# Planned durations of eight kinds of products, and the table of wanted times, in a kernel whose order of work is planned

## The chip, the cores and the metric

The kernel runs on one core of one Trainium2 chip, as one launch. The metric is the device time of a launch in microseconds (us). Before the change five runs took 1682.94 to 1686.12 us, with a median of 1685.28 us.

The core has five engines that matter here, each with a queue of its own that runs in the order written: TensorE (PE in the profile; PEld is its loading of weights), VectorE (DVE), ScalarE (ACT), GpSimd (POOL) and SyncE (SP, which starts most transfers).

## The reference, cut to what matters

A stream x of 64 sequences of 64 tokens of width 128 goes through four layers. Each layer adds, through a tanh gate, an attention to a context of width 96 and then a feed-forward part:

```python
x = x + tanh(g_xattn[0]) * L0_xattn(layernorm(x), ctx)      # 16 heads
x = x + tanh(g_ffn[0])   * L0_ffn(layernorm(x))             # 32 experts, 6 of them a token, and a shared one
x = x + tanh(g_xattn[1]) * L1_xattn(layernorm(x), ctx)      # 16 heads, clamp, NaN guard
x = x + tanh(g_ffn[1])   * L1_ffn(layernorm(x))             # 8 experts, 2 a token, and a shared one
x = x + tanh(g_xattn[2]) * L2_xattn(layernorm(x), ctx)      # 8 heads of 64
x = x + tanh(g_ffn[2])   * L2_ffn(layernorm(x))             # 8 experts, 2 a token, and a shared one
x = x + tanh(g_xattn[3]) * L3_xattn(ctx, layernorm(x), mask)  # resampler: 2 heads, keys of context and x
x = x + tanh(g_ffn[3])   * L3_ffn(layernorm(x))             # 4 experts, 2 a token, norms inside
```

All is float32. Attention stays inside a sequence, so blocks of sequences are independent of each other all the way down, except that layer 1's clamped attention has one NaN flag for all.

## The kernel before, in words

**Tiling.** The 4096 tokens are cut into 8 blocks of 512 (`NB`, `TOK`): four tiles of 128 tokens, 8 sequences. x stays in on-chip memory for the whole launch. A stage is one part of one layer for one block: `attention_16` (layers 0 and 1), `gated_ffn` (layers 0 and 2), `end_attention_1`, `sparse_ffn` (layer 1, for two blocks at a time, a group), `context_8` (keys and values of layer 2, which need x not at all, written to memory and read again), `attention_8`, `attention_lat` (layer 3) and `ffn_3`.

**Products.** Experts' weights are dense in layers 0 and 2: for each chunk of 128 hidden units TensorE makes g and u, ScalarE puts Silu on g (tile h), VectorE multiplies by u, GpSimd multiplies by the expert's weight pb in layer 0 (in layer 2 it scales the input beforehand), and TensorE adds the product to acc. The weights come from a route: logits (pl), scores and top-k on VectorE (tile c), a transpose (pcT), a copy (cT), a store to memory (cD) and a load that repeats one row over all partitions (pb). In layer 1 the route makes a table of slots (prank, then VectorE, then pid), GpSimd gathers the tokens (zs), the experts' weights come by transfers (wt), results go to memory (oD) and are gathered again (back). `ffn_3` makes its norm's variances by products (pg, pvar), then a transpose pt, a route (pcT with cr), a spread (pb, zs) and products ph and acc.

**Who decides the order.** No instruction is issued when the Python code reaches it. `Plan` records every operation (`note`), groups some into units that stay together (`unit`), and at the end `order` lays all of them on five queues in a list schedule: it steps through time, and an engine that is free takes, of the operations whose inputs are ready and whose tiles fit in the pools, the one with the smallest key. `issue` then writes the instructions in the order of their planned starts. The plan costs nothing on the chip: only the order remains of it, and each engine runs its own part of that order, waiting by semaphores for what it needs.

Two inputs of the plan are touched by the change. One is the planned duration of an operation: `_duration` works it out of engine and size, and `nc.unit(us)` puts a number in its place. So `with nc.unit(0.93, claim=[pr])` says that the four score products of a tile take TensorE 0.93 us. The units with a number are the scores (sc), the weighted sums (av) and the values (pv) of the attentions, pvar, and acc. The other is the key: `stage` gives each operation a wanted time between a start and an end, in proportion to the planned TensorE work of its stage done so far; start and end come from the table `TIMES`, by kind of stage and block. The numbers order the operations among each other; they need not be times that are kept.

Beside this the plan models hand-overs between engines (`HOP`), transfers, a port shared by VectorE and GpSimd, the change of ScalarE's function tables (`TABLE_LOAD`), a slower TensorE after a pause (`COLD`), and the number of buffers.

Since all instructions are issued by `bound(*args, **kw)` in `issue`, nearly all of them have one line in the profile, L435. They are told apart by the names of their tiles.

Of the kernel before, what the change touches and what calls it, by code (L numbers as in the profile page):

```python
# [47 lines left out]

TIMES = {
    "16 heads, 0": [  # L50
        (-54.5, 328), (250.4, 262.4), (374.9, 421.5), (506.5, 421.8),
        (569.6, 591.2), (622.8, 674.7), (713.4, 645.8), (778.3, 584.2),
    ],
    "16 heads, 1": [
        (333, 444.3), (423.8, 572.1), (557.3, 698.9), (649.7, 728.9),
        (528, 564.7), (824.1, 934.8), (897.1, 1004.8), (764.9, 1636.1),
    ],
    "8 heads": [
        (1784.4, -176.2), (1320.1, 880.9), (1496.5, 1065.9), (1635.3, 950.3),
        (1016.4, 1173.4), (1845.9, 1720.9), (1648.7, 1814.1), (2307, 1648.3),  # L60
    ],
    "context, 8 heads": [
        (-1147.3, -84.8), (477.4, 520.9), (377.6, 314.9), (633.9, 1171.7),
        (690.6, 791.4), (824, 1018.8), (1320.9, 1029), (1545.2, 1373.3),
    ],
    "end of 16 heads, 1": [
        (985.5, -185.1), (934.2, -12.1), (1624.5, 1208.6), (677.3, 370.2),
        (1548.3, 1684.6), (1613, 2357.5), (2268, 1506.6), (1257.7, 1182.8),
    ],
    "gated 0": [  # L70
        (374.1, 413.5), (399.2, 482.9), (487.5, 550.8), (555.8, 662.2),
        (639.4, 711.8), (705.7, 784.1), (771.6, 834.8), (824.4, 943.5),
    ],
    "gated 1": [
        (-14.1, 982.7), (998.8, 1329.4), (1464.1, 1777.1), (1740.3, 1898.3),
    ],
    "gated 2": [
        (-577.4, 810.8), (1063.5, 1347.3), (-255, 804.4), (709.7, 1264.9),
        (1127.4, 1220.7), (970.7, 1635.2), (271.5, 1477), (1190.9, 2021.9),
    ],  # L80
    "last": [
        (1168.5, 1372.8), (1313.9, 1442.4), (1334.7, 1838.8), (1476.8, 1489.4),
        (2151.3, 2352.2), (2115.9, 2719.1), (3058.2, 3370.9), (261.9, 602.3),
    ],
    "resampler": [
        (-938.8, 590.2), (409.2, 477.3), (251.8, 893.4), (1125.5, 1677.4),
        (-179.1, 1216.5), (691.6, 289.1), (1556.9, 1376.5), (684.3, 580.8),
    ],
}
AT_ONCE = {}  # L90
# [366 lines left out]
def flamingo_kernel(ctx: ExitStack, tc: tile.TileContext, a: dict, out: bass.AP):  # L457
    nc = Plan(tc)
# [285 lines left out]
    with nc.stage(0.0, 1.0):  # L744
        nc.gpsimd.memset(sums_w, 0.0)
        for i in range(2):
# [3 lines left out]
            t = tile_of([P, BB * 4, 2, 32], f"values{i}")  # L750
# [8 lines left out]
    def attention_16(layer, blk):  # L759
# [49 lines left out]
        def scores(pr, t):  # L809


            kb = tile_of([P, 2, 8, S], "kb")
            nc.gpsimd.tensor_mul(
                kb,
                kT[:, t * P : (t + 1) * P].rearrange("p (b s) -> p b s", s=S).unsqueeze(2).to_broadcast([P, 2, 8, S]),
                head8.unsqueeze(1).unsqueeze(3).to_broadcast([P, 2, 8, S]),
            )
            sc = ps_two("sc")
            with nc.unit(0.93, claim=[pr]):
                for b in range(2):  # L820
                    q0 = t * P + b * S
                    for h in range(2):
                        nc.tensor.matmul(
                            sc[b * 64 : (b + 1) * 64, h, :],
                            lhsT=qT[h * 64 : (h + 1) * 64, q0 : q0 + S],
                            rhs=kb[h * 64 : (h + 1) * 64, b, :, :],
                            start=True,
                            stop=True,
                        )
            sc_h = sc.rearrange("p h (j s) -> p (h j) s", s=S)  # L830
            top = tile_of([P, 16], "top")
            if layer == 1:

                T = blk * TB + t
                nc.scalar.activation(pr, sc_h, AF.Tanh, accum_out=seen[:, T : T + 1])
            nc.vector.tensor_reduce(top, sc_h, axis=AX.X, op=ALU.max)
            wide = top.unsqueeze(2).to_broadcast([P, 16, S])
            if layer == 1:

                nc.vector.tensor_scalar(top, top, CLAMP, -CLAMP, op0=ALU.min, op1=ALU.max)  # L840
                nc.vector.scalar_tensor_tensor(pr, sc_h, -CLAMP, wide, op0=ALU.max, op1=ALU.subtract)
                nc.vector.tensor_scalar_min(pr, pr, 0.0)
            else:
                nc.vector.tensor_tensor(pr, sc_h, wide, op=ALU.subtract)
            flat = pr.rearrange("p h s -> p (h s)")
            nc.scalar.activation(flat, flat, AF.Exp, scale=scale)
            done.append(len(nc.ops) - 1)

        def weighted(pr, t, acc_tile):

            acc = acc_tile.rearrange("p (i n) -> p i n", i=2)
            prT = tile_of([P, 8, P], "prT")
            for g in range(2):
                pt = ps("pt")
                transposed(
                    pt, [pr[:, 2 * j : 2 * j + 2, :].rearrange("p h s -> p (h s)") for j in range(4 * g, 4 * g + 4)],
                    claim=[prT, acc_tile],
                    behind=done[t | 1],
                )
                nc.scalar.copy(prT[:, 4 * g : 4 * g + 4, :].rearrange("p j q -> p (j q)"), pt)  # L860
            with nc.unit(1.2):
                for b in range(2):
                    cols_b = slice(t % 2 * P + b * 64, t % 2 * P + (b + 1) * 64)
                    for odd in range(2):
                        for c in range(4):
                            nc.tensor.matmul(
                                acc[32 * c : 32 * c + 32, 0, cols_b],
                                lhsT=of_pair(v[:, (2 * t + b) * 4 + c, :, :], odd),
                                rhs=prT[:, 2 * c + odd, b * 64 : (b + 1) * 64],
                                start=(odd == 0),  # L870
                                stop=(odd == 1),
                            )
                for odd in range(2):
                    for c in range(4):
                        nc.tensor.matmul(
                            acc[32 * c : 32 * c + 32, 1, t % 2 * P : (t % 2 + 1) * P],
                            lhsT=of_pair(sums_w, odd),
                            rhs=prT[:, 2 * c + odd, :],
                            start=(odd == 0),
                            stop=(odd == 1),  # L880
                        )
            if t % 2:
                rs = tile_of([P, 2 * P], "rs")
                nc.vector.reciprocal(rs, acc[:, 1, :])
                nc.vector.tensor_mul(yT[:, (t - 1) * P : (t + 1) * P], acc[:, 0, :], rs)
# [84 lines left out]
    def attention_8(blk):  # L970
# [22 lines left out]
        def softmax(pair):  # L993

            sc = ps_two("sc8")
            pr = tile_of([P, 8, 2, S], "pr8")
            with nc.unit(1.35, claim=[pr]):
                for t in range(2):
                    for j in range(4):
                        for h in range(2):  # L1000
# [26 lines left out]
        def weighted(pair, pr):  # L1027
            for t in range(2):
# [2 lines left out]
                transposed(pt, [pr[:, 4 * t + j, :, :].rearrange("p h s -> p (h s)") for j in range(4)], claim=[prT])  # L1031
                nc.scalar.copy(prT.rearrange("p j q -> p (j q)"), pt)
                av = ps("av8")
                with nc.unit(1.25, claim=[yT[2 * pair + t]]):
                    for b in range(2):
                        for j in range(4):
                            for h in range(2):
# [45 lines left out]
    def attention_lat(blk):  # L1083
# [19 lines left out]
        v = tile_of([P, BB, P], "v3")  # L1103
        for g in range(2):
            pv = ps("pv3")
            with nc.unit(1.05, claim=[v]):
                for b in range(4 * g, 4 * g + 4):
                    for h, (src, w) in enumerate(((cT, w3kv), (lT, w3lkv))):
                        nc.tensor.matmul(
                            pv[h * 64 : (h + 1) * 64, b % 4 * P : (b % 4 + 1) * P],  # L1110
                            lhsT=src[:, b * S : (b + 1) * S],
                            rhs=w[:, P : 2 * P],
                            start=True,
                            stop=True,
                        )
# [5 lines left out]
            )  # L1121
        sc = ps_two("sc3")
        pr = tile_of([P, 2, TB, P], "pr3")
        with nc.unit(1.3, claim=[pr, low]):
            for t in range(TB):
                for h in range(2):
                    hs = slice(h * 64, (h + 1) * 64)
# [26 lines left out]
            nc.scalar.copy(prT[:, h, :, :].rearrange("p t q -> p (t q)"), pt)  # L1154
        av = ps("av3")
        yT = tile_of([P, TOK], "yT3")
        with nc.unit(1.4, claim=[yT]):
            for t in range(TB):
                for b in range(2):
                    for h in range(2):  # L1160
# [170 lines left out]
    def gated_ffn(layer, blk):  # L1331
# [9 lines left out]
        for n, (i, who) in enumerate(chunks):  # L1341
# [17 lines left out]
            nc.vector.tensor_mul(h, h, u)  # L1359
            if who is not None and layer != 2:  # L1360
                nc.gpsimd.tensor_mul(h, h, pb)
            with nc.unit(0.95):
                nc.tensor.matmul(acc, lhsT=w2[:, w], rhs=h, start=(n == 0), stop=(n == len(chunks) - 1))
        add_to_x(blk, tokens_again(acc), gate_f(layer))

# [153 lines left out]
    def sparse_ffn(group):  # L1519
# [13 lines left out]
        for blk, zT in zip(blocks, zTs):  # L1533
            acc = ps("acc")
            for ch in range(chunks):
# [7 lines left out]
                    nc.tensor.matmul(u, lhsT=shared_w[:, 1, w], rhs=zT, start=True, stop=True)  # L1543
                nc.scalar.activation(h, g, AF.Silu)
                nc.vector.tensor_mul(h, h, u)
                with nc.unit(0.95):
                    nc.tensor.matmul(acc, lhsT=shared_w[:, 2, w], rhs=h, start=(ch == 0), stop=(ch == chunks - 1))
            add_to_x(blk, tokens_again(acc), gate_f(1))
        oD = dram.tile([SLOT_TILES * P, D], F32, tag="oD", name="oD")
# [127 lines left out]
    def ffn_3(blk):  # L1677
# [39 lines left out]
        for i in range(8):  # L1717
# [2 lines left out]
            with nc.unit(claim=[h, acc]):  # L1720
                nc.tensor.matmul(ph, lhsT=w1[:, i * P : (i + 1) * P], rhs=zs[i // 2], start=True, stop=True)
            nc.scalar.activation(h, ph, AF.Relu)
            with nc.unit(0.95):
                nc.tensor.matmul(acc, lhsT=w2[:, i * P : (i + 1) * P], rhs=h, start=(i == 0), stop=(i == 7))
        po = tokens_again(acc).rearrange("p (t d) -> p t d", d=D)
        mv, r = moments([po[:, t, :] for t in range(TB)], "on")
# [153 lines left out]
```

## Time and profile before

| | |
|---|---|
| median of 5 runs | 1685.28 us (1682.94 to 1686.12) |
| the profiled execution's own time | 1682.23 us |
| its span, first to last instruction | 1680.4 us |
| mean granted TensorE clock | 0.972 |
| TensorE busy | 1565.9 us (93%), 12737 instructions |
| VectorE busy | 1069.0 us (64%) |
| GpSimd busy | 969.5 us (58%) |
| ScalarE busy | 883.1 us (53%), of it 163 loads of function tables, 209.1 us |
| transfers | 180.74 MB, 108 GB/s on average |

The span is what the profile covers; the time of the execution has 1.83 us around it. Busy time of TensorE is the time in which some product is under way: products overlap, so a product's duration in the profile (603 ns for half of a 128x512 float32 product, which goes through the array in two passes) is longer than the distance from its start to the next one's. The granted clock is the share of full speed that the chip let TensorE run at; it is seen to switch between full and half. "A wait" is idle time of an engine ahead of an instruction, put down to the operation that ended it.

### The profile page before, as it was taken

The page shows a single profiled execution, that of the slowest core. Times are in us where ns is not written, and L with a number is a line of the kernel's source. Part 1 is how long each engine was busy: PE and PEld are TensorE (multiplying, and loading weights), DVE is VectorE, ACT ScalarE, POOL GpSimd, SP SyncE. Part 2 cuts the span into 40 slices and gives each one's busy share as a digit, 9 for nine tenths or more (in the row PEclk, how much of TensorE's full clock was granted, in tenths as well). Part 3 has the DMA queues.
Part 4 walks back from the last instruction along what each step waited for, and adds up shares of the span by engine and source line. Part 5 has one row for each costly group of instructions (what it writes and reads, how often), then busy time and mean ns, then how long its engine had stood idle before and what let it go on. Part 6 is the DMA issues. An engine that isn't in the chain of part 4 may idle for free.

```text
span 1680.4 us, 34191 instructions
## 1 busy us (share of the span) xinstructions
PE 1565.9 (93%) x12737; PEld 938.9 (56%) x12737; DVE 1069.0 (64%) x2932; ACT 883.1 (53%) x1325; POOL 969.5 (58%) x986
## 2 busy tenths in 40 slices
PE   5999999999999999998959999999999997999987
PEld 2645444454554554556848766757467665664543
DVE  3865577677867656676467657665766545665563
ACT  2654667676767645753325537565446543453522
POOL 8374655664564655523275768665478555955651
PEclk9999999999999999997979999999999999999998
DMA  7232234422321313134758554131344624121001
GB/s 236 93 109 65 77 94 152 128 91 68 78 94 49 111 44 120 54 133 157 209 188 219 183 163 133 60 110 40 119 133 123 214 24 159 38 77 51 33 15 56
DMA packets 107774, 180.74 MB, mean 108 GB/s; under 512 B 22964, under 2 KB 53016, under 8 KB 103128
## 3 DMA queue, kind: packets, MB, share of 16 engines
q1 hardware_dynamic: 102488, 168.06, 30.7%
q0 software_dynamic: 5120, 10.50, 3.2%
q8 instruction: 101, 1.65, 0.4%
q14 instruction: 65, 0.53, 0.1%
HBM read 146.71 MB, written 35.26 MB: 108 GB/s over the span
## 4 chain that ended last, share of the span: by engine, by line
PE 43%; POOL 7%; DMA 4%; DVE 4%; issue 2%; ACT 1%; SPq 0%; DVEq 0%; POOLq 0%; ACTq 0%
PE acc L435 7%; PE g L435 6%; PE u L435 6%; PE po L435 5%; PE pt L435 3%; PE av L435 3%; PE ph L435 2%; POOL z L435 2%; POOL back L435 2%; PE pv L435 2%; PE pk L435 2%; PE sc L435 2%; PE pq L435 1%; PE pg L435 1%; PE pz L435 1%
## 5 line engine op out<-in xcount | busy, mean ns | idle before, releaser
L435 POOL TENSOR_TENSOR h<-h,pb 128x512 f32<-128x512 f32 x128 | 162.2, 1281 | 181.3 <-DVE h L435 117.5
L435 DVE TENSOR_TENSOR h<-h,u 128x512 f32<-128x512 f32 x224 | 150.4, 683 | 180.1 <-PE u L435 133.1
L435 ACT ACTIVATE h<-g 128x512 f32<-128x512 f32 x224 | 132.2, 597 | 213.4 <-PE g L435 185.8
L435 ACT ACT_TABLE_LOAD x163 | 209.1, 1283 | 24.2 <-PE g L435 10.8
L435 POOL TENSOR_TENSOR ln_r<-ln_ve,minus_half 128x4 f32<-128x4 f32 x64 | 66.5, 1038 | 176.0 <-DVE ln_ve L435 173.5
L435 DVE TENSOR_REDUCE top<-sc 128x16 f32<-128x1024 f32 x80 | 97.3, 1217 | 82.2 <-PE sc L435 55.8
L435 POOL TENSOR_TENSOR kb<-kT,masks 128x1024 f32<-128x1024 f32 x64 | 121.3, 1909 | 41.5 <-ACT kT L435 30.2
L435 PE MATMUL u<-zTm,w_L 128*128 128x512 f32 x272 | 141.3, 602 | 2.0 <-DVE h L435 1.3
L435 PE MATMUL g<-zTm,w_L 128*128 128x512 f32 x272 | 141.6, 603 | 0.5 <-DVE h L435 0.5
L435 POOL DMA_INDIRECT zs<-zD,z_rows x96 | 95.8, 998 | 75.9 <-DVE z_rows L435 45.0
L435 PE MATMUL acc<-h,w_L 128*128 128x512 f32 x272 | 138.3, 608 | 0.0
L435 PE MATMUL acc<-h,L_w 128*128 128x512 f32 x272 | 135.2, 600 | 2.8 <-ACT h L435 2.1
L435 ACT COPY prT<-pt 128x512 f32<-128x512 f32 x176 | 96.3, 592 | 45.4 <-PE pt L435 45.0
L435 POOL TENSOR_TENSOR pb<-zTm,pb 128x512 f32<-128x512 f32 x64 | 81.9, 1304 | 50.6 <-DMA pb<-cD 44.8
L435 PEld LDWEIGHTS pt<-masks,pr 128*128 128x128 f32 x704 | 82.6, 143 | 48.3 <-issue 34.3
L435 ACT ACTIVATE pr<-pr 128x1024 f32<-128x1024 f32 x88 | 93.1, 1058 | 20.4 <-DVE pr L435 19.5
L435 PE MATMUL pt<-masks,pr 128*128 128x128 f32 x704 | 97.8, 280 | 1.6 <-POOL pr L435 1.6
L435 POOL DMA_INDIRECT back<-oD,rows_of x64 | 65.0, 1015 | 40.0 <-DMA oD<-zs 17.9
L435 DVE SCALAR_TENSOR_TENSOR x<-po,gates,x 128x512 f32<-128x512 f32 x56 | 41.7, 747 | 69.1 <-PE po L435 68.9
L435 PEld LDWEIGHTS u<-zTm,w_L 128*128 128x128 f32 x272 | 48.5, 191 | 58.1 <-issue 47.3
L435 PEld LDWEIGHTS g<-zTm,w_L 128*128 128x128 f32 x272 | 48.3, 190 | 57.8 <-issue 45.7
L435 POOL TENSOR_SCALAR z<-x,ln_mv,ln_r 128x128 f32<-128x128 f32 x96 | 76.8, 810 | 1.5
(300 smaller groups left out, 3490.6 us busy)
## 6 DMA issues: line engine op xcount, KB each, us to landing
wt<-experts SPq DMA_DIRECT2D x96, 384.0 KB
pb<-cD SPq DMA_DIRECT2D x256, 128.0 KB
pb<-cD SPq DMA_DIRECT2D x96, 256.0 KB
k_d<-kS SPq DMA_DIRECT2D x8, 1024.0 KB
v_d<-vS SPq DMA_DIRECT2D x8, 1024.0 KB
kT<-k_d SPq DMA_DIRECT2D x8, 1024.0 KB
v<-v_d SPq DMA_DIRECT2D x8, 1024.0 KB
oD<-zs SPq DMA_DIRECT2D x32, 192.0 KB
```

Of the source, the lines that this page charges most:

```text
L435: bound(*args, **kw)
```

## The change

Eight kinds of units get other planned durations, and `TIMES` gets other numbers throughout. Nothing else is edited: the operations, the tiles and the pools are the same.

| unit | TensorE products in it | units | before | after |
|---|---|---|---|---|
| sc, 16 heads | 4 | 64 | 0.93 | 1.10 |
| av, 16 heads | 24 | 64 | 1.20 | 1.10 |
| sc8, 8 heads | 32 | 16 | 1.35 | 1.20 |
| av8, 8 heads | 16 | 32 | 1.25 | 1.17 |
| pv3, resampler | 8 | 16 | 1.05 | 0.97 |
| sc3, resampler | 16 | 8 | 1.30 | 1.10 |
| av3, resampler | 16 | 8 | 1.40 | 1.17 |
| acc, all feed-forward parts | 1 | 288 | 0.95 | 0.86 |

```diff
 TIMES = {
     "16 heads, 0": [
-        (-54.5, 328), (250.4, 262.4), (374.9, 421.5), (506.5, 421.8),
-        (569.6, 591.2), (622.8, 674.7), (713.4, 645.8), (778.3, 584.2),
+        (-218.9, 180.8), (96.9, 222.5), (494.2, 524.3), (583.8, 558.6),
+        (674.4, 696.1), (725.7, 776.3), (814.1, 744.9), (887.2, 748),
     ],
...
     "last": [
-        (1168.5, 1372.8), (1313.9, 1442.4), (1334.7, 1838.8), (1476.8, 1489.4),
-        (2151.3, 2352.2), (2115.9, 2719.1), (3058.2, 3370.9), (261.9, 602.3),
+        (1294.4, 1457.3), (1383.4, 1568.8), (1409.3, 1950), (1146.2, 1322.8),
+        (2328, 2565.4), (1954.4, 2831.2), (2475.5, 3606.3), (-348.4, 879.3),
     ],
...
-            with nc.unit(0.93, claim=[pr]):
+            with nc.unit(1.1, claim=[pr]):
...
-            with nc.unit(1.2):
+            with nc.unit(1.1):
...
-            with nc.unit(1.35, claim=[pr]):
+            with nc.unit(1.2, claim=[pr]):
...
-                with nc.unit(1.25, claim=[yT[2 * pair + t]]):
+                with nc.unit(1.17, claim=[yT[2 * pair + t]]):
...
-            with nc.unit(1.05, claim=[v]):
+            with nc.unit(0.97, claim=[v]):
...
-        with nc.unit(1.3, claim=[pr, low]):
+        with nc.unit(1.1, claim=[pr, low]):
...
-        with nc.unit(1.4, claim=[yT]):
+        with nc.unit(1.17, claim=[yT]):
...
-            with nc.unit(0.95):
+            with nc.unit(0.86):
```

The last edit is made at three places: `gated_ffn`, the shared expert of `sparse_ffn`, and `ffn_3`. All ten kinds of stages in `TIMES` have new numbers for all their blocks.

In the issued program the same instructions stand in another order on every queue. With equal neighbours merged, TensorE's queue has 1863 rows before and 1853 after; VectorE's 2149 and 2137, ScalarE's 1055 and 1041, GpSimd's 548 and 551, SyncE's 663 and 662, and on each many of the rows moved. Only the loads of ScalarE's function tables change in number, from 163 to 156.

## The prediction

> **What bounds the kernel now.** First the head of the page and its slices over time: is one engine full, and where is it not?
>
> ```profile
> span 1680.4 us, 34191 instructions
> PE 1565.9 (93%) x12737; PEld 938.9 (56%) x12737; DVE 1069.0 (64%) x2932; ACT 883.1 (53%) x1325; POOL 969.5 (58%) x986
> PE   5999999999999999998959999999999997999987
> PEclk9999999999999999997979999999999999999998
> ```
>
> TensorE is busy 93% of the span and nothing else comes over 64%. So the span is TensorE's work plus the holes in it: 1680.4 - 1565.9 = 114.5 us of holes, and some time in which its clock is low. The holes sit at the start, at slices 18 to 21 and at the end. The windows of 40 us put numbers on them (columns: stretch, its length, then busy time and count of PE, PEld, DVE, ACT, POOL, then the granted clock, DMA share and GB/s):
>
> ```profile
> 0.00:40.00 40.00, 20.97 (x120) 9.85 (x120) 13.99 (x52) 11.37 (x18) 33.29 (x49) 0.95 0.77 237
> 80.00:120.00 40.00, 36.32 (x150) 16.31 (x149) 29.61 (x82) 20.15 (x29) 31.79 (x38) 0.96 0.31 93
> 360.00:400.00 40.00, 37.46 (x306) 19.02 (x306) 28.28 (x77) 26.75 (x37) 27.17 (x29) 0.96 0.12 40
> 840.00:880.00 40.00, 22.74 (x97) 16.84 (x97) 26.63 (x114) 9.81 (x15) 29.51 (x29) 0.70 0.57 197
> 1400.00:1440.00 40.00, 30.53 (x88) 14.34 (x87) 18.43 (x62) 10.39 (x16) 31.47 (x31) 0.91 0.45 162
> ```
>
> In the other stretches TensorE is at 36 to 40 of 40 us. What ends the holes is told by the waits of TensorE (total us, times, longest):
>
> ```profile
> PE pid L435 <- DVE match L435: 15.5, 2, 10.2
> PE pcT L435 <- DVE c L435: 8.3, 3, 3.7
> PE g L435 <- POOL pb L435: 8.2, 2, 7.9
> PE pt L435 <- DMA zs<-zD,z_rows: 6.6, 4, 4.4
> PE pbias L435 <- DMA L_gate<-in_L_gate: 5.7, 1, 5.7
> PE pvar L435 <- DVE q L435: 5.5, 2, 4.9
> ```
>
> Each is a routing chain (pid: slots of experts; pcT: expert weights; g after pb: weights spread over partitions; pvar: variances) that had too few other products queued behind its start. I call the sum of the products that stand in TensorE's queue between the start of such a chain and the product that waits for its end its **cover**. Covers are counted from the order of the queue with distances from the timeline: 0.86 us for a 128x512 product (u at 82.24, g at 83.11), 0.44 for four transposes (po at 81.37, pc at 81.81), 1.02 for four sc products (sc at 30.93, pc at 31.95).
>
> **The change, part by part.**
>
> *The durations.* They enter no instruction. In the plan they take off about 31 us of TensorE's work: 288 acc products x 0.09 = 25.9, the attention kinds 16.1, and sc gives 64 x 0.17 = 10.9 back. On the chip both kernels have the same 7113 products, 695 transfers of SP and 160 indirect ones of POOL. TensorE's work term is 0.
>
> *The table of ScalarE's functions* is loaded 156 times instead of 163: 7 x 1.283 us (ACT_TABLE_LOAD, 209.1 us for 163) = 9.0 us of an engine that is 53% busy. Taken as 0; if it stood on the path, -9.0.
>
> *The order* changes on every queue (TensorE, VectorE, ScalarE, GpSimd, SyncE). I compare covers at each hole.
>
> (a) Start. pbias, which waits for the fourth gate matrix, stands third in the queue before and behind pv after. These rows show what it held up:
>
> ```profile
> 15.63 0.56 PE L435 MATMUL pbias<-L_gate,shift 128*128 128x4 f32 x2 [5.73 <-DMA L_gate<-in_L_gate]
> 16.05 1.07 PE L435 MATMUL pc<-masks,c_in 128*96 128x128 f32 x4
> 27.41 0.60 PE L435 MATMUL pz<-masks,z 128*128 128x128 f32 x4
> 13.50 0.21 ACT L435 ACTIVATE gates<-rows 128x8 f32<-128x8 f32 x1 [11.47 <-DMA rows<-in_rows]
> 7.57 2.73 POOL L435 TENSOR_SCALAR c_in<-c_in,cn_mv,cn_r 128x96 f32<-128x96 f32 x4
> ```
>
> The centred c_in is there at 10.30, so pc can start 5.7 us earlier; but the copy cn is queued on ScalarE behind gates, which ends at 13.71, where it was at 17.15. So the front moves by 3.4, less 0.4 for pbias further on: -3.0. pz, at 27.41 - 3.0 = 24.4, is behind the end of z (18.9) still. Bounds: -5.7 and 0 (a later transfer takes over; SP's c_in load goes behind two context loads of 0.4 us, and its user is blocks away).
>
> (b) Layer-0 routes (eight). Covers between pl and pcT were 8.8, 7.0, 8.5, 7.5, 8.9, 9.3, 7.9, 14.4 us and become 11.2, 33.7, 13.1, 10.7, 20.9, 8.9, 8.8, 8.2. The chain's own VectorE work is about 7.2 us. Other VectorE work put inside it now is 3.7, 2.6 and 10.1 us in routes 2, 3 and 5, which have the covers for it. The two that waited (3.68 us in 80:120, 3.08 in 280:320) gain 2.4 and 3.2 of cover: -5.5. Bounds -6.8 and 0.
>
> (c) Layer-2 routes. The two that waited (1.41 and 1.55 us) get 1.0 and 1.9 more; two others lose 2.2 and 0.3 (to 3.0 and 3.7, where 4.1 is needed): -2.5 + 1.5 = -1.0. Bounds -3.0 and +2.
>
> (d) The hole of 7.92 us at 1407, in the last pair's routing. From pcT (1405.62) to g (1415.17) 9.55 us pass with 1.3 of products, and eight back gathers of 1.25 each stand on GpSimd ahead of pb. After, all 16 gathers come before the route, and 6.4 us of products, attention's av8 among them, lie inside. Of those, pt must itself wait for the softmax (cover 4.7 us, its chain 8.0): 3.3. So 7.92 - 3.3 = -4.6. Bounds -7.9 and 0.
>
> (e) Sparse groups 0 and 1: cover from prank to pid 4.3 to 5.2 and 0.9 to 2.6. In group 1 the gathers follow on GpSimd after 16 back gathers, so there the cover from the last po of group 0 to pt counts: 10.3 to 11.2. -0.9 each: -1.8. Bounds -4 and +1.
>
> (f) One hand-over pcT to ph: cover 5.3 to 9.5, and 1.3 us of wait go: -1.3 (-1.3 to 0).
>
> (g) The end. Before, the last attention output po starts at 1614.44 and the span ends 65 us after po, with 37.6 us of products in between. After, 34.9: 2.7 move ahead. But both last pcT-to-ph covers are now small (1.4 to 0.9 and 11.2 to 0.4 us), and a pcT-to-ph chain took 8.7 (1631.24 to 1639.91). By hand, counted from po: ph 7.4, pz 10, pg to 16.4, pvar 20.8, pt 23.5, pcT 28.3, ph 36, last acc 50 to 51.5, and then the 10.2 us that follow it now: 60 to 62. Against 65, less the 2.7: -0.3 to -2.3; I take -1.0. Bounds -3 and +6 (the last cover lost in full).
>
> (h) What is new. Chains counted alone, without queues: in TensorE positions 30 to 400 the products with less cover than their chain go from 6 to 28, missing 1.1 us before and 7.7 after. Before, such short ones in the first 600 us cost about what they miss (sc 0.86, u 1.26), so +5.0. Two attention transposes late in the kernel miss 1.6 and 1.5: +3.1. Bounds 0 and +20: products with under 1 us to spare go from 460 to 519, and 59 x 0.35 us (half of a plain hand-over, as ACT o to po 0.68) is 20.
>
> (i) The clock. 80:120 is at 0.96 with its hole, 1.6 us lost, and 280:320 likewise; 1400:1440 at 0.91, 3.6 us. With b and d half of this 6.8 comes back, 3.4, and the clock that short new waits cost is taken at 1.4: -2.0 (-6 to +3). For the new ones 360:400 is the row: 0.96 with no hole over 1.53 us, two of which follow close. The Trainium skill (TensorE: Matmul & The Clock Gate, Why this matters for your kernels) asks only for no idle gaps above about 3 us, and by it the new short waits would cost no clock; the window 360:400 differs, and the measurement decides. By the page the sum below would be -13.5; by the row it stays.
>
> Sum: -3.0 - 5.5 - 1.0 - 4.6 - 1.8 - 1.3 - 1.0 + 5.0 + 3.1 - 2.0 = -12.1 us. The profiled execution took 1682.23 us, 1.83 around the span, and stands 3.05 under the median 1685.28 of the runs; against it 1670.1, and against the median **1673 us**.
>
> **The rivals.**
>
> 1. Slower: the tighter queue decides. Other engines run in the order written, and a late VectorE result holds the queue behind it. Price: h at its upper end, +20 instead of +8.1, and the gains b and d half spent on it (+5): -12.1 + 11.9 + 5 = +5, and with the end at its upper bound (+7) +12: 1690 to 1697. It decides from about 0.3 us a product in those 59. For it: 22 products more in positions 30 to 400 have less cover than their own chain. Against: they miss 0.3 us each on average, and the stages 120 to 700 run at 36 to 40 of 40 us.
>
> 2. No change: one local optimum against another. The missing cover summed over all chains is 75.8 us before and 77.1 after, and sc's new 1.10 is over its distance of 1.02, so not all durations are the chip's: 1685 within 3.4.
>
> 3. Faster than forecast: new short waits are taken up by the queues (h at 0 to 2) and the clock stays up: -12.1 - 7 - 3 = -22: 1663.
>
> **How the numbers follow.** Forecast 0.50, range 1667 to 1681; rival 1 0.21, rival 2 0.11, rival 3 0.18. A difference of under 0.2% (3.4 us) can't be told from none here. Faster: 0.50 + 0.18 = 0.68; same 0.11; slower 0.21. The range for 8 in 10 leaves out the far half of rival 1 and of rival 3: 1657 to 1693.
>
> **What would show it.** Right: no wait at pbias before pc, pz before 25; no pcT wait over 1.5 us in the first 650 us; the 7.92 us hole under 4; TensorE idle near 100 us. At the end a wait of 5 to 8 us before the last ph and before the second but last. Wrong: many waits of 0.2 to 1 us in 30 to 400 with VectorE or ScalarE as releaser (rival 1), or DVE-bound slices that were not there. The weakest step is h: covers tell of chains alone, not of the queues of four engines.

## The result: slower, and the profile after

The changed kernel takes 1694.08 us (median; 1685.26 to 1702.5), the kernel before 1684.93 us in the same comparison: a ratio of 1.0054, 95% interval 1.0043 to 1.0064. It is slower by about 9 us, where 12 us of gain were forecast. The profiled execution spans 1692.9 us against 1680.4, with a mean granted clock of 0.967 against 0.972.

The head of the page and two of its rows over time:

```profile
span 1692.9 us, 34168 instructions
...
PE 1569.3 (93%) x12737; PEld 945.1 (56%) x12737; DVE 1071.9 (63%) x2932; ACT 872.8 (52%) x1318; POOL 963.6 (57%) x986
...
PE   6999999999999999998969889999999998999976
...
PEclk9999999999999999988969999999999999999988
```

TensorE is busy 3.4 us longer for the same products, which goes with its lower clock, and idle for 1692.9 - 1569.3 = 123.6 us instead of 114.5. Of the windows, four of the stretches shown of before and one more (columns as there):

```profile
0.00:40.00 40.00, 23.57 (x150) 11.35 (x154) 15.89 (x54) 13.14 (x21) 34.82 (x49) 1.00 0.79 242
80.00:120.00 40.00, 38.54 (x154) 18.45 (x153) 30.75 (x111) 23.01 (x33) 29.14 (x31) 1.00 0.43 139
360.00:400.00 40.00, 38.08 (x190) 16.33 (x189) 31.02 (x72) 32.25 (x45) 18.97 (x15) 1.00 0.29 94
960.00:1000.00 40.00, 32.68 (x334) 24.59 (x333) 26.47 (x85) 18.48 (x28) 27.88 (x29) 0.91 0.49 152
1400.00:1440.00 40.00, 34.51 (x383) 21.72 (x382) 31.82 (x120) 16.03 (x26) 31.73 (x34) 0.99 0.19 57
```

The places that the prediction named did get better: 80 to 120 by 2.2 us, 1400 to 1440 by 4.0. Longer windows show where TensorE is idle instead. The last column is a second profile of the same changed kernel, taken with the experiments; it tells how far one profile can be trusted:

| stretch, us | before | after | after again |
|---|---|---|---|
| 0 to 120 | 23.2 | 21.2 | 22.0 |
| 120 to 720 | 9.2 | 16.6 | 16.1 |
| 720 to 960 | 31.6 | 30.6 | 31.3 |
| 960 to 1080 | 4.7 | 11.2 | 7.5 |
| 1080 to 1440 | 18.1 | 11.0 | 10.2 |
| 1440 to the end | 27.8 | 33.0 | 34.4 |

The waits of TensorE (total us, times, longest):

```profile
PE ph L435 <- DVE zs L435: 15.6, 2, 8.0
PE pid L435 <- DVE match L435: 13.4, 2, 8.1
PE pt L435 <- DMA zs<-zD,z_rows: 12.4, 8, 4.7
PE sc L435 <- DVE pr L435: 10.9, 11, 2.6
...
PE pcT L435 <- DVE c L435: 5.1, 5, 1.6
PE pt L435 <- POOL pr L435: 4.4, 9, 1.2
```

The long route waits shrank (pcT from 8.3 to 5.1, pid from 15.5 to 13.4). New are the two waits of ph at the end, twice as much waiting for gathered tokens (zs, 6.6 before; 8.9 in the second profile), and many small ones: sc had 4.1 us in 4 waits.

Idle time alone does not place the loss, because the stretches hold different work. A point that both orders reach with almost the same work behind them is the first pid, which begins the slots of layer 1: 6096 product records of 12737 are done there before, 6071 after. From there to the end, before and then after:

```profile
771.90:1680.40 908.50, 837.27 (x6642) 565.20 (x6642) 543.00 (x1708) 415.65 (x657) 546.99 (x580) 0.96 0.37 114
```

```profile
771.80:1692.90 921.10, 844.87 (x6666) 572.28 (x6666) 550.21 (x1709) 411.87 (x655) 541.51 (x580) 0.95 0.37 113
```

Up to the first pid the two kernels take the same time, 771.9 and 771.8 us (774.2 in the second profile): after is idle 4.1 us more there and busy 4.1 us less. The whole 12.5 us between the two spans lie behind it: 5.0 us more idle time, and 7.6 us more of busy time for nearly the same products. So the change did two things, and they have to be explained apart: in the first stages its gains were eaten up, and in the later ones it lost time.

### The profile page after: what moved, and what is told of

Read it like the earlier page. It is cut to its first block, busy times and chain, and to the rows that moved or that the text cites. A ratio compares the mean times of both kernels' runs of the same rounds, so it can differ in the third digit from the quotient of the medians.

```text
span 1692.9 us, 34168 instructions
## 1 busy us (share of the span) xinstructions
PE 1569.3 (93%) x12737; PEld 945.1 (56%) x12737; DVE 1071.9 (63%) x2932; ACT 872.8 (52%) x1318; POOL 963.6 (57%) x986
## 3 DMA queue, kind: packets, MB, share of 16 engines
q8 instruction: 101, 1.65, 0.4%
## 4 chain that ended last, share of the span: by engine, by line
PE 68%; DVE 11%; POOL 7%; issue 5%; DMA 5%; ACT 3%; SPq 1%; POOLq 0%; DVEq 0%; ACTq 0%
PE acc L435 13%; PE g L435 11%; PE u L435 11%; PE pt L435 5%; PE po L435 5%; PE av L435 5%; PE sc L435 4%; PE ph L435 3%; PE pk L435 3%; PE pv L435 2%; DVE top L435 2%; DVE pr L435 2%; PE pq L435 2%; DMA pb<-cD 2%; POOL z L435 1%
## 5 line engine op out<-in xcount | busy, mean ns | idle before, releaser
L435 DVE RECIPROCAL rs<-av 128x256 f32<-128x256 f32 x32 | 56.1, 1753 | 40.1 <-PE av L435 40.1
L435 PE MATMUL ph<-zs,L_w 128*128 128x512 f32 x128 | 66.6, 644 | 15.6 <-DVE zs L435 15.6
L435 PE MATMUL sc<-kb,qT 64*64 64x512 f32 x512 | 70.2, 618 | 11.5 <-DVE pr L435 7.3
```

## The experiments

**The suspect in the first stages.** Between 120 and 720 us the waits of TensorE name ScalarE and VectorE tiles one by one, mostly for 1 to 3 us. One step further back they have something in common. ScalarE's waits for GpSimd's h in this stretch, before and after:

```profile
ACT h L435 <- POOL h L435: 4.6, 4, 2.3
...
ACT zTm L435 <- POOL h L435: 1.5, 1, 1.5
...
ACT zTs L435 <- POOL h L435: 1.1, 1, 1.1
```

```profile
ACT h L435 <- POOL h L435: 11.4, 4, 4.1
...
ACT qT L435 <- POOL h L435: 6.8, 3, 3.2
```

7.2 us before, 18.2 after. The timeline of after at the longest of them (start, duration, engine, operation, idle time before it and what ended that):

```profile
437.13 3.12 POOL L435 TENSOR_SCALAR z<-x,ln_mv,ln_r 128x128 f32<-128x128 f32 x4
...
440.33 1.28 POOL L435 TENSOR_TENSOR x<-x,bo 128x512 f32<-128x512 f32 x1
...
441.57 3.76 POOL L435 TENSOR_TENSOR kb<-kT,masks 128x1024 f32<-128x1024 f32 x2
...
445.29 3.72 POOL L435 TENSOR_TENSOR h<-h,pb 128x512 f32<-128x512 f32 x3
...
446.58 0.60 ACT L435 ACTIVATE h<-g 128x512 f32<-128x512 f32 x1 [4.12 <-POOL h L435]
...
447.23 1.13 PE L435 MATMUL pk<-c,L_k 96*128 96x512 f32 x2 [2.80 <-ACT h L435]
```

GpSimd works without a pause (19.15 of 20 us from 436 to 456; 7.47 in before): layernorm's z, a bias, two kb for an attention to come, and only then the multiplies of h by the experts' weights. ScalarE's next h waits 4.12 us for the first of these, presumably for its buffer, and TensorE, which waits for ScalarE, 2.80. The wait is three engines long, and no cover counted from a product's own inputs sees it.

**Four orders: mixed pairs and small nudges.** The first two kernels exchange one of the change's two halves each; the other two move each number of a table a little.

```diff
 # mixed pairs: TIMES of one kernel, the eight nc.unit(us) of the other
 # nudges: TIMES = {k: [(a + r(), b + r()) ...]}, r uniform in -0.3..0.3 (before), -1..1 (after)
```

> The eight new durations with the old table of wanted times. Theory 1, the durations themselves cost time (with 0.09 us less for each acc and 0.03 to 0.23 less for the attention kinds, sc apart, TensorE's products are planned closer behind their inputs): slower than before by at least the 9 us that the whole change cost, 1694 to 1720, with many short waits in 120 to 720 us, where before had 9.2 us of TensorE idle and after has 16.6. Theory 2, a table is worth something only with the durations it was found for, whichever these are: slower by much more than the change, 1710 to 1770, with holes of 5 us and more at route chains, not short waits. If the durations were harmless and only the new table bad: 1685 or faster.

> The eight old durations with the new table. Theory 1 (the durations cost, the table gives): faster than after, under 1690. Theory 2 (the pair counts): slower than both kernels, 1710 to 1770, with long holes at route chains, as in the other mixed pair. If the table alone were bad: 1694 or more, but with the same holes as after (15.6 us at the last two ph, 12.4 us at the gathered tokens).

> Before, with every number of its table moved by up to 0.3 us at random, the durations left. About a fifth of TensorE's queue is then in another order. Theory 3, the 9 us are the luck of one order against another that is as good by its planner: this moves the time by as much as the change did, 3 to 15 us up or down, 1670 to 1700. If the order is not that touchy: 1685 within 3.4.

> After, with every number of its table moved by up to 1 us at random, the durations left; nearly every stretch of the queues then has another order. Theory 1 (the shorter durations make any order tight): 1694 within 6, and TensorE's idle time in 120 to 720 us again about 16 us. Theory 3 (luck of one order): anywhere from 1675 to 1715, with the idle time in 120 to 720 between 9 and 25 us and the long holes at other places.

These four ran on another chip, on which before itself took 1737.68 us. The nudged before shows where: it reaches the first pid at 771.6 us, as before does on the other chip, and the rest is slower. Only the ratios and the stretch 120 to 720 are compared.

| kernel | ratio to before | 95% interval | TensorE idle, 120 to 720 |
|---|---|---|---|
| new durations, old table | 1.0541 | 1.0498 to 1.0584 | 26.3 |
| old durations, new table | 1.0277 | 1.0254 to 1.0300 | 15.7 |
| before, nudged | 0.9992 | 0.9971 to 1.0014 | 8.9 |
| after, nudged | 1.0079 | 1.0053 to 1.0105 | 19.6 |

Both mixed pairs are slower by much more than the change, so a table is tied to the durations it was found for, and the parts can't be added. The nudges speak against theory 3 as far as they go: before stayed where it was, and after was again slower, by 0.8%, with 19.6 us of idle time and 25 us of ScalarE waiting for GpSimd's h. But they go less far than was expected of them. In the traces, with equal neighbours merged, 277 of 1900 rows of TensorE's queue are in another order than in before, and only 237 of 1888 than in after, none of these between 360 and 540 us and none behind 712. So the loss survives a nudge; that it belongs to all orders of this kind is not shown.

**One queue.** Three kernels on a chip where before takes 1683.63 us: after again; after with half of each weight multiply left out; after with GpSimd's own order changed and nothing else.

```diff
 # half multiply: layer 0, order frozen
-                    bound(*args, **kw)             # gpsimd.tensor_mul(h, h, pb)
+                    bound(h[:, :256], h[:, :256], pb[:, :256])
 # weights first: GpSimd's queue only, after the order is made
+  for each POOL op "h<-h,pb": while the POOL op ahead of it is a kb
+      and that kb starts, by the plan, after the inputs of h are there:
+          move h ahead of it
```

> The changed kernel itself, beside the others of this call, as their base: 1.0054 times before, as measured. In the runs of the mixed pairs before took 1737.68 us where it had taken 1685, with the loss behind 720 us; if that comes back, the stretch 120 to 720 must still show about 16.6 us of TensorE idle time.

> After, with the same order on every queue, but GpSimd multiplies only half the columns of each hidden tile h by its expert weight in layer 0 (128 multiplies of 1.27 us become shorter; the other half stays unweighted). Theory A, GpSimd's queue is what made the first stages lose: in 120 to 720 us ScalarE waited 18.2 us for GpSimd's h in after and not at all in before, and TensorE behind it. Then these waits go under 4 us, TensorE's idle time in 120 to 720 falls from 16.6 to 8 to 11, and the time by 5 to 9 us below after. Theory B, the products are simply too close behind VectorE's and ScalarE's results: the idle time stays within 2 us of 16.6 and the time within 3 us of after.

> After, with one queue alone in another order: on GpSimd a multiply of h by its weight goes ahead of the kb multiplies (1.91 us each) that stand before it, where its inputs were planned to be there by then. Nothing is left out. Theory A: the 18.2 us of ScalarE's waits for GpSimd's h in 120 to 720 us fall by half or more, TensorE's idle time there falls from 16.6 to about 12, and the time by 3 to 6 us, unless the scores that need kb now wait (kb is late by 1.3 to 3.8 us; each such wait gives 1 us back). Theory B: no change beyond 2 us in either direction.

One figure in these texts is wrong: ScalarE did wait for GpSimd's h in before, 7.2 us as shown above; TensorE hardly felt it.

| kernel | median us | ratio to before | ACT waits for POOL h | TensorE idle, 120 to 720 | first sc to first pid, us | first pid to the end |
|---|---|---|---|---|---|---|
| after again | 1694.84 | 1.0058 (1.0036 to 1.0080) | 18.2 | 16.1 | 745.0 | 920.1 |
| half multiply | 1685.08 | 1.0002 (0.9986 to 1.0018) | 15.0 | 14.3 | 735.5 | 921.1 |
| weights first | 1685.11 | 1.0003 (0.9987 to 1.0019) | 4.0 | 11.7 | 734.5 | 921.2 |

With the weights first, the place shown above becomes:

```profile
437.70 1.28 POOL L435 TENSOR_TENSOR x<-x,bo 128x512 f32<-128x512 f32 x1
...
438.94 3.72 POOL L435 TENSOR_TENSOR h<-h,pb 128x512 f32<-128x512 f32 x3
...
440.24 0.60 ACT L435 ACTIVATE h<-g 128x512 f32<-128x512 f32 x1 [0.41 <-POOL h L435]
...
441.63 0.59 PE L435 MATMUL pk<-c,L_k 96*128 96x512 f32 x1
```

The three multiplies stand ahead of the two kb, ScalarE waits 0.41 us instead of 4.12, and pk follows without a wait. The order of GpSimd's queue in layer 0 is worth 1694.84 - 1685.11 = 9.7 us, as much as the change lost. Theory A holds in kind and exceeds its size (3 to 6 us): between the first score and the first pid 10.5 us went, of which 5.2 were idle time and 5.3 are shorter busy time. Against the first profile of after, which took 742.5 us there, it is 8.0 us, 6.2 of them idle time.

But the 9.7 us are not the same microseconds that the change lost. From the first pid to the end after takes 920 to 921 us with the weights first or not, and before 908.5. (That profile of before is 2.7 us under the median; five others of before's orders whose later stages were left as they were take 907.9 to 914.6, and the nudged after with the weights first, below, takes 913.7 in a run 5 us under its median.) The weights first win in the first stages what the change loses in the later ones. The fault on GpSimd explains why the first stages gained nothing; the loss behind the first pid stays, and no run removes it.

Half the multiply agrees in time (9.8 us) but with the signs of neither theory: ScalarE's waits fell only to 15.0 us and TensorE's idle time by 2.6 of the 9.5 us between the first score and the first pid; the other 6.9 are shorter busy time. Against the first profile of after it is 3.7 of 7.0 us, so how much of it is the clock depends on the profile that is taken as base. Nor do ScalarE's waits alone tell the cost: in a run below (before's order, new durations) they are 11.8 us, and TensorE is idle for 8.5 in that stretch, less than in before.

Rows of 240 to 260 us of after and of the half multiply:

```profile
240.00:260.00 20.00, 18.16 (x152) 9.03 (x152) 7.27 (x8) 7.49 (x13) 14.54 (x10) 0.83 0.64 200
```

```profile
240.00:260.00 20.00, 18.68 (x218) 9.51 (x209) 9.17 (x11) 9.67 (x16) 12.97 (x12) 1.00 0.72 223
```

In after a wait of 1.84 us before u, from 244.8 us on, is followed by a clock of 0.83; with the same wait at 1.31 us the clock stays at 1.00.

**Does the rule carry over?** The same rule on the nudged after, on before as a control, and on after together with two more moves.

```diff
 # three moves = weights first, and
+  POOL: gathers zs<-zD ahead of the gathers back<-oD before them, where z_rows was planned to be there
+  SP:   L_k, L_v of layer 2 ahead of the four L_gate
```

> The other order of after (table moved by up to 1 us), in which ScalarE waited 25 us for GpSimd's h between 120 and 720 us and TensorE was idle there for 19.6 us (1.0079 times before), with the same rule on GpSimd: multiplies of h ahead of kb. Theory A, GpSimd's turn costs any order of this planner's shorter durations: the idle time falls to 12 to 14, the ratio to 0.998 to 1.002. Theory B, the gain in after was the luck of one order: ratio 1.005 or more.

> The control: before, with the same rule on GpSimd (multiplies of h ahead of kb). In before ScalarE waited 7.2 us for GpSimd's h in 120 to 720 us, and TensorE behind it for 0.7 us at most. Theory A: nothing to win, 0.999 to 1.001; what kb loses may cost 1 to 3 us. If the rule is good whatever the order: 0.996 or less.

> After with the weights first on GpSimd, as in the run before (1.0003 times before), and two moves more. (1) On GpSimd the gathers of tokens (zs) of layer 1 go ahead of the gathers of results (back) that stand before them, where their table was planned to be there: the waits for zs of 1.46 and 0.91 us at 964 to 967 in after (1.78 us at the same place with the weights first) should go, 2 to 3 us; the products that use the back results may take some of it again. (2) On SyncE the matrix L_k of layer 2, for which pk waits 1.72 us at 17 us in after, is fetched ahead of the four gate matrices: 1 to 2 us. Together -3 to -5 us against the weights first alone: 0.997 to 0.9985 of before. If GpSimd's turn matters only in layer 0: 1.000.

The nudged after goes from 1.0079 to 1.0023 (1.0007 to 1.0039), its idle time from 19.6 to 12.0: about seven tenths of its loss, a little short of the 1.002 that theory A allowed; the two ratios are from different chips, and this order has most of its rows in common with after's. The control is slower, 1.0021 (1.0008 to 1.0035): there was nothing to win in before, and the rule costs 3.5 us. It is no good rule by itself; it mends a fault that after's order has.

The three moves gave 1.0060 (1.0039 to 1.0081), by the medians 7 us more than the weights first alone. The gathers did it: without them, in a run below, the other two moves give 0.9994. In the timeline, VectorE and TensorE behind the results (back) that now come later:

```profile
865.89 0.18 DVE L435 CAST rows_of<-both 128x16 int32<-128x16 f32 x1 [10.04 <-DMA back<-oD,rows_of]
...
870.50 0.55 DVE L435 TENSOR_TENSOR hs<-hs,u 128x384 f32<-128x384 f32 x1
...
871.21 0.77 PE L435 MATMUL po<-wt,hs 128*128 128x128 f32 x2 [4.33 <-DVE hs L435]
```

The wait for zs near 860 fell from 4.73 to 2.87 us, and those at 964 to 967 all but went. But VectorE waited 10.04 us for back with hs queued behind it, and TensorE has four new waits of 4.33, 1.65, 3.24 and 4.08 us. From the second to the third pid the run took 63.1 us instead of 57.5.

**The start.** Term a alone, in before; then with the transfer that took its place.

```diff
 # before_pbias_later: TensorE's queue
-  pf pf pbias pc pk pv
+  pf pf pc pk pv pbias
 # before_start: the same, and on SyncE
+  L_k, L_v of layer 2 ahead of the four L_gate
```

> Before, with one product moved: pbias, which waits 5.73 us for the fourth gate matrix at the start, goes from third in TensorE's queue to behind the first pv, where the changed kernel has it. Term a of the prediction says -3.0 us, bounds -5.7 and 0. If the front is taken up by a later wait (the scores for qT, which wait 2.11 us at 32 us): 0. In after the start stretch 0 to 40 had 2.6 us more of TensorE's work than in before.

> Before with pbias behind the first pv, as in the run that gained nothing, and on SyncE the matrices L_k and L_v of layer 2 ahead of the four gate matrices. In that run pk waited 3.60 us at 17.6 us for L_k, just what pbias had freed. If this transfer is the whole reason that term a gave nothing: the scores sc start at 27.5 to 28.5 us instead of 30.9 and the time falls by 2.5 to 3.5 us, 0.998 of before. If the front is held by something else (z, kb): 1.000.

```profile
13.14 2.07 PE L435 MATMUL pk<-cn,L_k 97*128 97x512 f32 x2 [2.03 <-ACT cn L435]
...
21.25 6.31 PE L435 MATMUL pk<-c,L_k 96*128 96x512 f32 x8 [3.60 <-DMA L_k<-in_L_k]
27.39 0.60 PE L435 MATMUL pz<-masks,z 128*128 128x128 f32 x4
```

With pbias moved, the first pk starts at 13.14 us instead of 17.79, and the next pk then waits 3.60 us for L_k: pz starts at 27.39, where it was at 27.41. The time is 0.9997 of before (0.9981 to 1.0013). With L_k fetched earlier, the scores start at 29.32 instead of 30.93 and the ratio is 0.9992 (0.9976 to 1.0007); here pk waited 3.68 us for cn. The scores come 1.6 us earlier where 2.4 to 3.4 were expected, and the time can't be told from before's.

**Durations or table?** The mixed pairs could not say. So one kernel's planned starts are made the keys, and the plan is made a second time with the other durations. Where the durations stay, the order comes back: in the run with new durations in the first stages only, TensorE's queue behind 825 us is before's.

```diff
+    def again(self):
+        self.order()
+        for op, s in zip(self.ops, self.starts):
+            op.key = s
+        SWITCH = 0.0
+        # exchange the eight durations: all (first two runs), or only
+        # sc, av of the 16 heads and acc of layer 0 (last two runs)
+        return self.order()
```

> Before's own order as the wanted times (each operation's key is its planned start in before), planned a second time with the eight new durations. The queues stay close to before's, with half of their stretches shifted somewhere. Theory 1, the shorter durations take away slack that the chip needs: slower than before by 5 us or more, and TensorE's idle time in 120 to 720 us up from 9.2 to 13 or more. Theory 2, the durations are harmless and the table placed the work badly: within 4 us of before, idle time 8 to 11.

> After's own order as the wanted times, planned a second time with the eight old durations. Theory 1: faster than after by 4 us or more (1.003 of before or less), idle time in 120 to 720 us down from 16.6 to 12 or less. Theory 2: as after or slower, 1.004 or more, idle time 15 or more.

> After with the weights first on GpSimd and L_k, L_v of layer 2 fetched ahead of the gate matrices; the gathers stay where they are. The weights first gave 1.0003 of before; the earlier L_k let the first scores start at 27.8 us instead of 29.3 in the run with three moves: 1.5 us. So 0.999 of before, 0.9975 to 1.0005. If the loss of the run with three moves (1.006) came from the earlier L_k and not from the gathers: 1.004 or more.

> Before's own order as the wanted times, with the new durations only for sc and av of the 16-head attentions and for acc of layer 0; TensorE's queue differs from before's in its first 200 of 1863 rows alone. With all eight new durations the stretch from the first score to the first pid took 731.0 us against 741.0 in before, idle 18.4 against 21.9. If the corrected durations are good where they stand and only the later order was spoilt: that stretch at 730 to 734 again, the rest as in before, 0.993 to 0.997 of before. If the 10 us were paid back by the transfers and gathers behind it (those depend on when layer 1 begins): 0.998 to 1.002. Theory 1, shorter durations cost slack: 1.002 or more.

> The same with pbias behind the first pv and L_k, L_v of layer 2 ahead of the gate matrices, which let the first scores start 1.4 us earlier in before: 1.4 us less than the run above, 0.992 to 0.996 of before; if the two gains do not add, as above.

| kernel | median us | ratio to before | TensorE idle, 120 to 720 | first sc to first pid, us | first pid to the end |
|---|---|---|---|---|---|
| before (profiled run) | 1682.23 | | 9.2 | 741.0 | 908.5 |
| before's order, new durations | 1698.81 | 1.0093 (1.0065 to 1.0122) | 8.5 | 731.0 | 933.5 |
| after's order, old durations | 1711.21 | 1.0158 (1.0127 to 1.0188) | 17.0 | 748.2 | 934.0 |
| after, weights and L_k | 1684.40 | 0.9994 (0.9976 to 1.0012) | 11.7 | 734.7 | 920.8 |
| before, new durations in the first stages | 1678.90 | 0.9980 (0.9963 to 0.9997) | 9.0 | 734.1 | 911.6 |
| the same and the start | 1673.94 | 0.9952 (0.9936 to 0.9968) | 9.3 | 732.2 | 911.2 |

Theory 1 falls on both sides. With before's order the new durations leave the idle time of the first stages at 8.5 us and shorten them by 10 us; with after's order the old durations leave it at 17.0. What makes the first stages of after idle is the order that its table gives, not the numbers of the durations. The time of theory 1 came true on before's side, but not for its reason. Theory 2 has the idle time right on both sides and the time on after's (1.0158), but not on before's: before's order ends 13.4 us slower although its first stages gained 10. After's order ends 17 us above after. In before's order the loss shows as two waits of 7.7 us for gathered tokens at 852 to 861 us and one of 10.8 us for pb at 1416, so behind the first stages; presumably the long chains there lost the products that had covered them. After's order lost 6 us ahead of the first pid (777.7 against 771.8) and 13 behind it; why was not followed up.

So the corrected durations were then given to the first stages only. In the trace about 230 of 1900 rows of TensorE's queue differ from before's; all but two lie ahead of 700 us (they are not the first 200 rows, as the expectation has it). That gains 0.2%, less than the 0.3 to 0.7% expected if the durations are good where they stand: the first stages are 6.9 us shorter in the profiled runs, of which about 4 arrive. With the start as well it gains 0.48%, 1673.94 against 1683.13 us: faster than both kernels. The two gains do more than add (0.2 and 0.08% alone, the latter not told from none), though the intervals leave room for plain addition. The weights first with the earlier L_k, on after, ends level with before.

## Why the prediction was wrong

Two steps failed: h, the price of the new short waits, and i, the clock, with the waits of layer 1 that term e did not count. They failed in different places.

Ahead of the first pid the terms (a, b, the first part of h and some of i) come to about -4 us; measured are -0.1 and, in the second profile, +2.3. There h is the step: idle time in 120 to 720 rose by 9.3 us besides pcT, and the runs on GpSimd's queue show the reason, weights that stand behind two kb hold ScalarE and through it TensorE. Without that the stretch from the first score to the first pid is 8.0 to 10.5 us shorter.

Behind the first pid the other terms come to about -8 us; measured are +12.5 and +11.6. Of the 12.5, 7.6 are busy time, the term i, which the prediction put at a gain: TensorE's clock is at half speed for 65 us there before and for 88 and 94 us in the two profiles of after. The other 5.0 are idle time, with the gathered tokens of term e, the scores (sc for pr, +3.5) and g for q (+2.4) against what d and e won. What in the order causes this is not shown; the only run that tried the gathers made it worse.

Rival 1 gave 1690 to 1697 and the right sign. Its reason, a late result that holds the queue behind it, is what the runs show for the first stages, though the engine in front was GpSimd and not VectorE, and its price for the end did not fall due. That its time came true is in part luck: the first stages cost nothing against before, and the loss came from the later ones, for which it gave no reason but the end.

- **Durations and TensorE's work, 0:** right. Both traces have 12737 product records, and the busy time differs by 3.4 us.
- **Table loads, 0:** right; 7 fewer loads, no wait that names them.
- **a, -3.0:** the scores start 1.6 us earlier (29.32 against 30.93), pz at 25.8 and not before 25. The named bound "a later transfer takes over" is what happened: L_k holds the front, for 1.72 us in after and 3.60 in before with pbias moved, where the gain was nothing at all.
- **b, -5.5:** the two waits of pcT, 6.76 us together, became 1.46 and 1.24: -4.1. Right in kind; none over 1.5 us in the first 650.
- **c, -1.0:** waits of 2.96 us before, 2.98 after: 0, inside the bounds.
- **d, -4.6:** the 7.92 us hole is gone. Waits of g for pb fell from 8.2 to 3.6 us, -4.6, but the 3.6 is another hole, at 1056 us in an earlier route, which the prediction does not list (2.9 and another of 1.7 in the second profile).
- **e, -1.8:** pid -2.1, right. But groups 2 and 3 were not counted: waits for gathered tokens rose from 6.6 to 12.4 us, +5.8, nearly all of it at 960 to 985; in the second profile to 8.9, +2.3. The three-moves run shows that they can't be had back by turning the gathers round as it did.
- **f, -1.3:** no wait of ph is left before the end. Right.
- **g, -1.0:** from the last attention's po to the end 65.96 us before, 66.85 after: +0.9, inside the bounds. The two waits before ph are 7.95 and 7.68 us, as foretold.
- **h, +5.0 and +3.1:** idle time in 120 to 720 without pcT went from 6.1 to 15.4 us, +9.3 instead of +5.0. The prediction's own count of what chains miss, 7.7 - 1.1 = 6.6, would have been nearer; it booked 5.0 and does not say why. The second part, transposes that wait for POOL pr, cost +2.8. The weak place was the one the text named, chains counted alone. The largest wait of the stretch, 2.80 us at pk, ends with ScalarE's h, which is no input of pk at all.
- **i, -2.0:** TensorE's products took 3.4 us more instead, 4.1 less ahead of the first pid and 7.6 more behind it. The spells at 80 and 360 went as expected, and new ones came at 240 to 260 (0.83) and, behind the first pid, at 985, 1060, 1156, 1596 and 1664 us, against one at 1412 that went.

The terms as measured give -1.6 - 4.1 - 4.6 - 2.1 + 5.8 + 0.9 + 9.3 + 2.8 + 3.4 = +9.8, with f and small waits not assigned, against +12.5 between the two profiled spans. They come from one profile each; the second profile of after moves some of them by 2 to 4 us. The gains that were looked for were sized fairly, 12.4 of the 14.9 us claimed for a, b, d and e; what was wrong was the belief that the new waits cost about what their own chains miss, and that the clock would gain.

On the clock, the row and the rule. After the 1.84 us wait the clock is at 0.83 from 240 to 260 us in both profiles of after, and before it nothing longer than 1.03 us stands in 24 us. The Trainium skill (TensorE: Matmul & The Clock Gate, Why this matters for your kernels) asks for no idle gaps above about 3 us; by it this spell would not be there. The measurement decides, and the prediction's choice to price short waits by the row was right in direction and too small in size.

## What to carry to other kernels

When a kernel's order is changed, don't price a new short cover by its own chain; follow the wait back through the queues of the other engines to the instruction that holds a buffer, and look at an engine that is busy without a pause there even if its share of the span is 57%. When the repair of a fault wins back just what a change lost, check that it is the same stretch: here a point that both orders reach with the same work done showed that it was not. An input that other choices were tuned on, like a planned duration, is worth testing with the old choices kept as far as possible: here correcting three durations where they act first, with the rest of the order held, won 0.2%, where correcting all with a new table lost 0.5%. Changing the suspected order on one queue alone separates that queue from all others.

## What was not expected of the hardware

- Two chips ran the same kernel at 1684 and 1738 us. From the first score to the first pid the nudged before took 741.3 us on the slower chip and before 741.0 on the other; the difference lies behind, in the stages with gathers and transfers of weights (963.7 against 908.5 us). What makes it was not found.
- A wait of 1.84 us was followed by a clock of 0.83 over 20 us, the same wait at 1.31 us by none, and one of 2.80 us by none in one run of after and by 0.91 from 440 to 460 in another. The clock records of the traces go far to explain it. In each run the clock changes only at steps of 3.41 us, and where these steps lie differs from run to run. The 1.84 us fell into one step, whose next was at half speed; the 2.80 us were split 1.19 and 1.61 between two steps in the first profile and 0.86 and 1.95 in the second, and only the 1.95 was followed by half speed. Over all 19 traces, after a step at full speed with TensorE idle for 60% or more of it the next was at half speed in 164 of 164 cases; with less than 35% idle in 9 of 8201; in between it went either way. In these traces it is the share of such a step that counts, so one wait of 2.8 us across two steps may cost no clock, and the same order can have another clock in the next run.
- Shortening a multiply by half on an engine busy 57% of the span took 9.8 us off a kernel bound by TensorE at 93%, though between the first score and the first pid TensorE's idle time fell by only 2.6 or 3.7 us, by which profile of after is taken; the rest of the 9.5 or 7.0 us there is shorter busy time.
